# Two convolutional layers on one core: which bands of the last image have their third channel tile filtered on TensorE, and where the late taps stand

## The chip, the cores and the metric

The kernel runs on one core of one Trainium2 chip. The metric is the device time in microseconds of one execution; the figure given for a kernel is the median of its runs. The engines are called PE (TensorE's matrix multiply), PEld (its weight loads), DVE (VectorE), ACT (ScalarE), POOL (GpSimd) and SP (SyncE), as in the profile.

## The reference, cut to what matters

Eight images of 384 channels on a 64 x 64 grid pass through two layers, each added to its own input after a group normalisation:

```python
x = x + L0(gn(x), ...)   # linear attention with rotary positions
x = x + L1(gn(x), ...)
# L1:
t = einsum('bchw,oc->bohw', x, w_in)
t = irfft2(rfft2(8x8 blocks of t) * fft_filter)
t = conv 3x3, one filter for each channel (w_dw), zero padding
x1, x2 = t[:, :192], t[:, 192:]
out = einsum('bchw,oc->bohw', gelu(x1) * x2, w_out)
```

The edit concerns the 3 x 3 filter for each channel (the depthwise convolution) of the second layer in the last image.

## The kernel before, in words

All data are float32. The 384 channels lie in three tiles of 128 partitions. An image is cut into eight bands of eight rows (512 positions). For images 0 to 6 the second layer runs together with the keys of the next image; in the last image there is no next one, and a loop of its own (L1003 to L1023) runs over the eight bands. For each band j it calls, in this order:

- `expand_filter` (L618): the 1x1 convolution `w_in` on PE (`pi`, L624, 24 instructions in the profile), copies by ACT (`ht`, L631), the forward 8 x 8 transform on PE (`pd`, L638), and four multiplications by the filter on DVE (`tf`, L646).
- `normalised` for band j + 1 on ACT (`hf`, L332).
- `back_transform` (L649): the inverse transform on PE (`pb`, L659), copied by ACT into one of two ring buffers (L669). A ring buffer has ten rows, the band's eight and one on each side: row 0 is copied from the band before (L674), and row 9 of the band before is copied from this band's first row (L675). So a band's last row of filter taps can be made only when the next band has been transformed.
- `first_taps` (L702): tap k = 0 of each channel tile on ACT (L706).
- `contract` of band j - 2 (L779): the last 1x1 convolution `w_out` on PE (`pw`, L747 and L758), whose results ACT copies (`y`, L772) and POOL adds to the output by DMA (L777), or in the last band DVE adds (L774).
- `taps` of band j - 1 (L711): taps k = 1 to 8 on DVE (L720), one multiply-and-add of 128 x 512 for each tap and tile, 24 for a band. Taps 6 to 8 read row 9.
- `gate_taps` of band j - 1 (L722): GELU on ACT (L726, L730) and the product on DVE (L727, L731), into the single buffer `gated`, which must have been read by the `pw` of the band before.

For some bands (`on_array`, L681) the third channel tile is not filtered by ACT and DVE but by PE: nine matmuls with diagonal weights (`diagonals`, L685) add up in one PSUM bank (`ptap`, L694), and the gate reads that bank. In the kernel before these are bands 6 and 7 of the last image. Band 6's taps 0 to 5 stand in its `first_taps`, its taps 6 to 8 in `taps`, which is called after `first_taps` and `contract` of the next band; band 7 has all nine in `first_taps`. In the profile each of these matmuls is two instructions.

The calls above are not the order in which an engine works. A scheduler that runs when the program is built orders each engine's instructions by priority and by its own estimate of times, and so interleaves bands: each engine then runs its list in this fixed order, waiting where an operand isn't there. That list is part of the built program and can be read for both kernels without running them.

## Time and profile before

| | |
|---|---|
| runs | 3429.32, 3433.61, 3430.04 us |
| median | 3430.04 us |
| the profiled execution's own time | 3431.62 us |
| its span, first to last instruction | 3428.8 us |
| mean granted PE clock | 0.994 |
| last image's second layer (first `hf` to the last instruction of DVE) | 3248.8 to 3422.3 us |
| one DVE tap (L720), from one to the next when nothing is waited for | 0.667 us |
| taps on PE (L694), instructions | 36 |

The profile is of one execution, and its times are counted from the span's start. An engine's row gives how long it was busy; the arrow at a row's end names what ended the idle time before it. The granted clock is 1.00 when TensorE runs at full speed and 0.50 when it is held to half.

### The profile page before, as it was taken

Reading aid. Unit: us, or ns where it says so; the run is one execution under the profiler, and the core shown is the slowest. Engines: PE = TensorE matmul, PEld = TensorE weight load, DVE = VectorE, ACT = ScalarE, POOL = GpSimd, SP = SyncE. Lnnn points to the kernel's source line nnn. Section 1 sums busy time; section 2 is a strip of 40 time slices with the busy share of each in tenths; the row PEclk is TensorE's granted clock in tenths of the full one; section 3 lists DMA queues with packets and bytes.
Section 4 is the critical chain, followed back from the end, with each engine's and each line's share of the span. In section 5 each row is a group of like instructions: output and inputs, shape, how many; then the busy total and the mean of one; then the engine's idle time right before and its main releaser. Section 6 shows DMA issues by size and latency. Waiting matters only on the chain.

```text
span 3428.8 us, 50015 instructions
## 1 busy us (share of the span) xinstructions
PE 3337.2 (97%) x19760; PEld 1866.2 (54%) x19760; DVE 2801.2 (82%) x4396; ACT 1958.6 (57%) x3869; POOL 140.2 (4%) x247
## 2 busy tenths in 40 slices
PE   8999999999999999999999999999999999999988
PEld 5545555455654556545565455654556445564454
DVE  6586888869898698986989869897698967989598
ACT  4445666456655567545665557555576455554553
POOL 0000001000010000100001000010000000000000
PEclk9999999999999999999999999999999999999999
DMA  6323234333243333442343423334243331333113
GB/s 219 113 90 108 70 107 97 124 118 80 78 108 122 109 84 88 106 127 93 84 105 99 126 93 93 100 97 124 84 111 89 102 121 47 83 85 96 61 25 51
DMA packets 149328, 335.60 MB, mean 98 GB/s; under 512 B 27125, under 2 KB 38246, under 8 KB 140902
## 3 DMA queue, kind: packets, MB, share of 16 engines
q1 hardware_dynamic: 123702, 282.65, 24.8%
q0 software_dynamic: 25200, 49.55, 9.2%
q8 instruction: 155, 2.54, 0.3%
q14 instruction: 79, 0.65, 0.1%
q10 hardware_dynamic: 192, 0.21, 0.0%
HBM read 232.51 MB, written 99.88 MB: 97 GB/s over the span
## 4 chain that ended last, share of the span: by engine, by line
PE 64%; DVE 28%; ACT 5%; issue 2%; DMA 0%; SPq 0%; DVEq 0%; ACTq 0%
DVE dw L720 17%; PE pf L606 15%; PE pq L527 13%; PE acc L447 10%; PE pk L432 8%; PE pi L624 6%; PE pw L747 3%; PE pb L659 2%; DVE kc L439 2%; PE pd L638 2%; PE pw L758 1%; DVE kc L339 1%; DVE kc L435 1%; ACT ring L669 1%; PE pn L565 1%
## 5 line engine op out<-in xcount | busy, mean ns | idle before, releaser
L720 DVE SCALAR_TENSOR_TENSOR dw<-ring,w_dw,dw 128x512 f32<-128x512 f32 x1520 | 1061.4, 744 | 179.3 <-ACT ring L675 137.7
L432 PE MATMUL pk<-wk,x 128*128 128x384 f32 x1536 | 547.2, 495 | 8.7 <-DVE kc L435 8.7
L527 PE MATMUL pq<-x,wq 128*128 128x512 f32 x1152 | 520.8, 599 | 4.0 <-ACT qs L554 3.9
L606 PE MATMUL pf<-qc,mt 128*128 128x512 f32 x1152 | 513.6, 599 | 0.0
L624 PE MATMUL pi<-w_in,hf 128*128 128x384 f32 x1536 | 510.8, 489 | 2.1 <-ACT hf L332 1.3
L447 PE MATMUL acc<-xk,kc 128*128 128x385 f32 x1488 | 504.0, 492 | 0.0
L624 PEld LDWEIGHTS pi<-w_in,hf 128*128 128x128 f32 x1536 | 290.4, 191 | 204.9 <-issue 5.1
L447 PEld LDWEIGHTS acc<-xk,kc 128*128 128x128 f32 x1488 | 276.4, 190 | 204.5 <-issue 22.8
L432 PEld LDWEIGHTS pk<-wk,x 128*128 128x128 f32 x1536 | 278.1, 190 | 197.5 <-issue 22.8
L527 PEld LDWEIGHTS pq<-x,wq 128*128 128x128 f32 x1152 | 211.9, 190 | 255.1 <-issue 240.7
L606 PEld LDWEIGHTS pf<-qc,mt 128*128 128x128 f32 x1152 | 213.0, 190 | 250.0 <-issue 232.8
L399 ACT COPY xk<-px 128x384 f32<-128x384 f32 x248 | 118.1, 486 | 324.5 <-PE px L398 324.5
L631 ACT COPY ht<-pi 128x384 f32<-128x384 f32 x256 | 120.2, 479 | 235.7 <-PE pi L624 235.1
L610 DVE SCALAR_TENSOR_TENSOR x<-pf,bfc,x 128x512 f32<-128x512 f32 x192 | 140.9, 742 | 106.8 <-PE pf L606 106.2
L435 DVE TENSOR_TENSOR kc<-pk,kbias 128x384 f32<-128x384 f32 x256 | 141.2, 552 | 86.9 <-PE pk L432 85.6
L747 PE MATMUL pw<-gated,w_out 128*128 128x256 f32 x768 | 183.9, 386 | 5.7 <-DVE kc L435 5.6
L337 ACT ACTIVATE qs<-qc 128x1536 f32<-128x1536 f32 x64 | 95.0, 1484 | 158.0 <-DVE qc L556 148.0
L554 ACT ACTIVATE qs<-pq,qbias 64x512 f32<-64x512 f32 x128 | 87.3, 682 | 168.1 <-DVE qc L540 167.2
L179 ACT ACTIVATE differences<-x,shift 128x512 f32<-128x512 f32 x168 | 119.9, 714 | 77.1 <-DVE x L610 77.1
L777 POOL DMA_DIRECT2D out_dram<-y x63 | 80.7, 1281 | 2019.2 <-ACT y L772 1938.7
L669 ACT COPY ring<-pb 128x256 f32<-128x256 f32 x384 | 115.8, 406 | 81.3 <-PE pb L659 81.3
L747 PEld LDWEIGHTS pw<-gated,w_out 128*128 128x128 f32 x768 | 141.8, 192 | 33.6 <-DVE kc L435 11.3
(157 smaller groups left out, 4354.3 us busy)
## 6 DMA issues: line engine op xcount, KB each, us to landing
tq<-in_tq SPq DMA_DIRECT2D x64, 1024.0 KB, 4.8
x<-in_x SPq DMA_DIRECT2D x64, 768.0 KB, 6.3
tk<-in_tk SPq DMA_DIRECT2D x64, 768.0 KB, 4.5
out_dram<-x SPq DMA_DIRECT2D x63, 768.0 KB, 3.3
out_dram<-y POOLq DMA_DIRECT2D x63, 768.0 KB, 7.9
xs<-in_x SPq DMA_DIRECT2D x56, 768.0 KB, 5.8
wk<-in_wk SPq DMA_DIRECT2D x8, 576.0 KB, 3.9
wv<-in_wv SPq DMA_DIRECT2D x8, 576.0 KB, 3.7
```

Of the source, the lines that this page charges most:

```text
L179: nc.scalar.activation(out[:, m, :], x_[:, m, :], AF.Identity, bias=shift[:, m : m + 1], accum_out=of_m[0])
L432: nc.tensor.matmul(pk[:, :C], tokens(t), wks[:, t, :], start=(t == 0), stop=(t == CT - 1))
L435: nc.vector.tensor_add(kc[:, i, :], pk[:, :C], bias)
L447: nc.tensor.matmul(acc[m][:, : C + 1], kf[:, i, m * P : (m + 1) * P], xk[:, i, :], start=(j == 0 and i == 0), stop=(j == NBAND - 1 and i = ...
L527: nc.tensor.matmul(p_, wqs[:, t, m * P : (m + 1) * P], xt[b, j][:, t, :], start=(t == 0), stop=(t == CT - 1),)
L606: nc.tensor.matmul(p_, mt[:, t, m * P : (m + 1) * P], q[:, t, :], start=(t == 0), stop=(t == CT - 1))
L610: nc.vector.scalar_tensor_tensor(xm, p_, bfc[:, m : m + 1], xm, ALU.add, ALU.add)
L624: nc.tensor.matmul(p_[:, :C], h[:, t, i * P : (i + 1) * P], w_in[:, t, :], start=(t == 0), stop=(t == CT - 1),)
L631: nc.scalar.copy(ht[:, i, :], p_[:, :C])
L669: nc.scalar.copy(rows[:, u], ps[u][:, m - m0].rearrange("p s i (r c) -> p r s i c", r=8))
L720: nc.vector.scalar_tensor_tensor(acc[:, m], src, wd, acc[:, m], ALU.mult, ALU.add)
L747: nc.tensor.matmul(p_[h][:, m - m0, :], w_out[:, 0, m * P : (m + 1) * P], gated[:, h * HT : (h + 1) * HT], start=(m == m0), stop=False,)
```

## The change

Band 3 of the last image joins the bands whose third tile is filtered on PE. And the late taps (6 to 8) of such a band are called earlier: between `back_transform` and `first_taps` of the next band, so ahead of the next band's own taps, instead of in `taps`.

```diff
     def on_array(b, j):
 
-        return b == nb - 1 and j >= NBAND - 2
+        return b == nb - 1 and j in (3, NBAND - 2, NBAND - 1)
...
         t, acc = ring[j % 2], dw[b, j]
-        if on_array(b, j) and j < NBAND - 1:
-            array_taps(b, j, range(6, 9))
         for m in range(CT - on_array(b, j)):
...
         back_transform(b, j, tf[0])
+        if j and on_array(b, j - 1):
+
+            array_taps(b, j - 1, range(6, 9))
         first_taps(b, j)
         if j >= 2:
             contract(b, j - 2)
```

In the built order of the changed program, band 3's taps 0 to 5 stand on PE between its `pb` and `pw` of band 1; its taps 6 to 8 stand within `pw` of band 2. Band 6's taps 6 to 8 stand after the first of band 7's nine. On DVE, band 3 has 16 taps in place of 24; ten of them stand before `tf` of band 4 and six after it. Before `tf` of band 5 stand 15 taps of band 4, and before `tf` of band 6 stand nine of band 5's. The orders of POOL and SP are the same in both programs.

## The prediction

> **What bounds the kernel now.** I read the page first, then only the last image's second layer, since the edit acts from its band 3 on (after about 3310 us).

> ```profile
> PE 3337.2 (97%) x19760; PEld 1866.2 (54%) x19760; DVE 2801.2 (82%) x4396; ACT 1958.6 (57%) x3869; POOL 140.2 (4%) x247
> PE 64%; DVE 28%; ACT 5%; issue 2%; DMA 0%; SPq 0%; DVEq 0%; ACTq 0%
> ```

> PE bounds the whole, but the edited stretch may differ. Busy time by window (columns: PE, PEld, DVE, ACT, POOL, granted clock, DMA share, GB/s):

> ```profile
> 3268.00:3300.00 32.00, 28.31 (x299) 17.35 (x298) 30.82 (x50) 21.07 (x46) 1.28 (x1) 1.00 0.06 5
> 3300.00:3332.00 32.00, 26.00 (x284) 16.83 (x283) 31.82 (x53) 16.16 (x37) 1.28 (x1) 0.89 0.30 47
> 3332.00:3364.00 32.00, 29.62 (x211) 18.52 (x213) 31.78 (x51) 17.42 (x40) 2.55 (x2) 0.95 0.30 41
> 3396.00:3430.00 34.00, 23.24 (x96) 14.36 (x96) 19.69 (x32) 8.78 (x23) 2.83 (x3) 0.91 0.39 69
> ```

> Here DVE is full (31.8 of 32 us) until about 3367, then it is not. The DVE timeline tells what it waits for when it does wait:

> ```profile
> 3273.84 1.94 DVE L646 TENSOR_TENSOR tf<-pd,filt 128x384 f32<-128x384 f32 x4
> 3275.70 2.31 DVE L720 SCALAR_TENSOR_TENSOR dw<-ring,w_dw,dw 128x512 f32<-128x512 f32 x3
> 3279.00 6.05 DVE L720 SCALAR_TENSOR_TENSOR dw<-ring,w_dw,dw 128x512 f32<-128x512 f32 x9 [0.98 <-ACT ring L675]
> 3310.49 12.00 DVE L720 SCALAR_TENSOR_TENSOR dw<-ring,w_dw,dw 128x512 f32<-128x512 f32 x18
> ```

> Of a band's 24 taps (three tiles, k = 1 to 8), 15 need only the band itself; 9 (k = 6 to 8) need ring row 9, which L675 copies out of the next band. Here DVE had used up its 15 and waited. Row 9 is complete 5.13 us after the next band's tf started (3273.84 to 3278.97). A tap costs 12.00/18 = 0.667 us.

> The chain of waits after 3367 (us at, us long):

> ```profile
> 3366.99 0.57 DVE tf L646
> ...
> 3371.98 7.61 PE ptap L694 x12
> 3379.59 2.59 PE pw L747 x12
> 3382.18 1.50 PE pw L758 x12
> 3383.68 7.94 PE pi L624 x24
> 3391.61 0.89 PE pd L638 x8
> ...
> 3392.52 1.03 DVE tf L646 x2
> ...
> 3397.46 8.00 PE ptap L694 x18
> ```

> From the start of band 6's tf (3366.99) on, PE and its short hand-overs set the end. So the change is judged by one number: when does tf of band 6 start?

> [...]in the fence above nine taps stood still for row 9.[...] the granted clock was 0.50 in 3370 to 3374, and 12 tap matmuls took 7.61 us (634 ns each) against 18 in 8.00 us (444 ns) later.

> **Part 1: band 3's third tile to TensorE.** Removed: 8 DVE taps x 0.667 = 5.33 us and one ACT first tap (L706, 0.756; ACT has slack). Added: 9 taps = 18 matmul instructions x 0.444 = 8.0 us of PE, more when cold. Bank, ring and ptap gate reads (0.42 to 0.43 on DVE either way) cost nothing visible. POOL's and SP's orders are unchanged. Six of the taps stand between pb and pw of band 3; three stand among the pw of band 2, behind row 9. I walk the engine orders of the changed program with durations of the trace.

> Band 3. tf ends at 3310.57 as before. pb follows 0.94 later, ring copies (1.76), row 0 (0.24): ptap starts at 3313.55. PE has been idle some 2 us after small matmuls, as ahead of band 6's ptap[...]: 12 x 0.444 = 5.33 (low end), 7.61 (high end, as band 6's); taken 7.05, end 3320.6. Then the queue behind it: pw 2.59 + 1.50, pi 7.94, pd to tf 0.91: tf of band 4 can start at 3333.5. It started at 3327.34 in the trace.

> DVE meanwhile: 19 taps from 3310.49, the gate's multiply (held to 3323.9 by pw, then ACT's GELU), 4 taps, two half gates (0.9), then 7 taps of band 3: 3332.8. It waits 0.7 for tf, runs it (1.87), and has nothing left but band 3's six row-9 taps: 10 of 16 are done. Row 9 comes at 3333.5 + 5.13 = 3338.7. Stall: 3.3 us. This is the wait that takes the place of the removed taps; before, unfinished taps filled it.

> Band 4. 6 row-9 taps to 3342.7; a tap, the gate multiply (its GELU waits for pw of band 2, which PE ends at 3342.2 behind the three taps: just in time), 2 + 1 + 11 taps and two half gates: 3354.2. PE would have had tf of band 5 ready at 3343.7 + 7.94 + 0.91 = 3352.6, so DVE decides: tf at 3354.2 (before: 3347.04). All 15 own taps of band 4 are used up again. Row 9 at 3359.3; stall 3.3 us.

> Band 5. 7 row-9 taps, gate (0.6), 4 taps (2.67), half gates (0.9): 3368.1. Now the order puts **seven taps of band 5 ahead of tf of band 6** (in the kernel before there were only three of them before it). 7 x 0.667 = 4.67: tf starts at 3372.8, though PE is ready at 3370.1. Shift: 3372.8 - 3366.99 = 5.8. One tap stands amid the four tf: +0.67. Sum 6.5.

> Check by DVE's own account: -5.33 for 8 taps, +7.2 idle (0.7 at tf, twice 3.25 at row 9), six more taps of band 5 done before tf +4.0: +5.9.

> From here DVE's lead is worth nothing, because the PE chain follows tf at fixed distances: those six taps, done early, buy only idle time later (by this walk DVE is free at 3394.9 while tf of band 7 comes at 3399.0).

> **Part 2: the three taps of band 6 ahead of band 7's.** Before: ptap 8.00, pw 4.1, ptap 2.77, pw 4.1. After: 24 ptap instructions x 0.444 = 10.65, pw, pw: the same PE sum. What lay between pw of band 5 and of band 6 was cover for the gate of band 6 (GELU 0.63 after pw's L747 part, multiply 0.68). Without it these 1.35 us are covered by pw's L758 part (1.50) alone, and DVE has 6 + 15 taps from row 9 (14.0 us) in front of the multiply: pw of band 6 starts about 0.2 late. Between -0.1 and +1.0; taken +0.2.

> **Sum.** +6.5 + 0.2 = +6.7. Unknown: band 6's ptap warm (-2.3) or cold as before (0), taken -0.3; band 5's pb cold, row 9 late (0 to +0.5, band 4's was 5.67 in the trace), taken +0.3; hand-overs of about 0.04 on some eight steps that I left out, +0.3. Total +7.0. The profiled execution took 3431.62 (span 3428.8 and 2.8 around it), 1.6 over the median of 3430.04; its own sum would be 3438.6, and on the median the forecast is 3437.0.

> **Rivals.**
> 1. *The relief counts (faster).* DVE is full from 3268 to 3367 and 5.33 us leave it; if tf of band 6 comes earlier by that and PE then stays warm in its ptap (-2.3), the time is 3430.0 - 7.6 = 3422.4. It decides where tf of band 6 starts before 3366.99. Against it: row 9 can't come earlier than tf + 5.1, and PE has 8 us more to do between two tf with only 2 to 3.6 us of idle time in each band.
> 2. *PE becomes the bound, no more.* If DVE catches up and tf of band 6 starts when PE is ready (3370.1): +3.1 + 0.67 + 0.2 = +4.0, 3434.0. For it: ptap of band 3 warm pulls every later step 1.5 us forward. Against it: seven taps stand in front.
> 3. *All is hidden:* 3430. Speaks for it that the end is PE's chain; against it that this chain starts from the tf that moves.

> **Chances.** 0.2%, 6.9 us, is about what a measurement of this kernel can tell from no change; my forecast lies right at this line. Forecast mechanism 0.82 (+5 to +9: 0.52 over the line, 0.30 under it); rival 2 0.08 and rival 3 0.05, both within; rival 1 0.05, of which 0.04 by over 0.2% and 0.01 within. So faster 0.04, same 0.44, slower 0.52. The range takes both ptaps warm (+3) at its low end, and both fully cold with late rows and a spread of 1 to 2 us between runs at its high end (+10): 3433 to 3440.

> **What would show it.** Right: DVE idle for about 3 us ahead of six and of seven dw taps, released by ring L675; tf of bands 4, 5, 6 at about 3333.5, 3354, 3373; ptap of band 3 at about 3313.5 with a half clock in part; DVE busy falling well under 31.8 in 32 us between 3332 and 3364. Wrong: no such stalls, or tf of band 6 not later than 3369; then the walk missed slack on DVE. A ptap of band 6 at 5.3 us would alone take off 2.3.

## The result and the profile after

| | before | after |
|---|---|---|
| median of the compared runs (6 and 6) | 3431.28 us | 3443.74 us |
| lowest to highest | 3429.32 to 3433.61 us | 3442.71 to 3445.35 us |
| profiled execution's own time, span | 3431.62, 3428.8 us | 3443.7, 3441.9 us |

The changed kernel is slower by 12.5 us: ratio 1.0037, 95% interval 1.0025 to 1.0049. The forecast was +7.0, its range +3 to +10. The direction and the place were forecast, the size was not.

The two lines of the page that the prediction started from, for the changed kernel:

```profile
PE 3347.5 (97%) x19778; PEld 1869.5 (54%) x19778; DVE 2797.8 (81%) x4388; ACT 1962.8 (57%) x3868; POOL 140.3 (4%) x247
PE 64%; DVE 28%; ACT 5%; issue 2%; DMA 0%; SPq 0%; DVEq 0%; ACTq 0%
```

PE has 18 instructions more, as written, but 10.3 us more busy time (3347.5 against 3337.2). Eighteen at 0.444 us would be 8.0. DVE has eight instructions fewer. The shares of the chain are the same to the per cent: on the whole page the loss cannot be seen.

By stretch of time (columns as before: PE, PEld, DVE, ACT, POOL, granted clock, DMA share, GB/s):

```profile
3300.00:3332.00 32.00, 25.93 (x178) 15.34 (x177) 30.15 (x49) 11.86 (x27) 1.28 (x1) 0.84 0.22 28
3332.00:3364.00 32.00, 29.50 (x310) 18.07 (x308) 24.96 (x41) 18.68 (x42) 1.28 (x1) 1.00 0.29 47
3364.00:3396.00 32.00, 27.13 (x181) 15.69 (x180) 28.97 (x46) 13.23 (x31) 1.79 (x2) 0.84 0.17 25
3396.00:3430.00 34.00, 32.02 (x211) 18.73 (x210) 22.36 (x36) 11.32 (x28) 2.37 (x4) 0.95 0.25 32
```

DVE, full from 3332 to 3364 before (31.78), is now busy 24.96 us there: 6.8 us of new waiting. The clock is lower in the first row (0.84, it was 0.89). In the second it is full (0.95 before): the half clock has moved to other places.

The DVE timeline shows the waiting, row by row (start, length, what, how many, and in brackets the idle time before the row and what ended it):

```profile
3335.45 1.95 DVE L646 TENSOR_TENSOR tf<-pd,filt 128x384 f32<-128x384 f32 x4 [0.26 <-PE pd L638]
3340.62 4.72 DVE L718 SCALAR_TENSOR_TENSOR dw<-ring,w_dw,dw 128x512 f32<-128x512 f32 x7 [3.22 <-ACT ring L675]
3349.00 7.63 DVE L718 SCALAR_TENSOR_TENSOR dw<-ring,w_dw,dw 128x512 f32<-128x512 f32 x11
3356.66 1.95 DVE L646 TENSOR_TENSOR tf<-pd,filt 128x384 f32<-128x384 f32 x4
3361.84 4.72 DVE L718 SCALAR_TENSOR_TENSOR dw<-ring,w_dw,dw 128x512 f32<-128x512 f32 x7 [3.23 <-ACT ring L675]
3370.75 4.73 DVE L718 SCALAR_TENSOR_TENSOR dw<-ring,w_dw,dw 128x512 f32<-128x512 f32 x7
3375.39 1.02 DVE L646 TENSOR_TENSOR tf<-pd,filt 128x384 f32<-128x384 f32 x2
3402.80 1.95 DVE L646 TENSOR_TENSOR tf<-pd,filt 128x384 f32<-128x384 f32 x4 [3.58 <-PE pd L638]
```

The two stalls at row 9 are there, 3.22 and 3.23 us (forecast: 3.3 twice), and so are the seven taps ahead of tf of band 6, without a wait between them and it. The part that was wrong is found on PE. The chain of waits of the changed kernel:

```profile
3315.08 7.43 PE ptap L694 x12
3322.51 2.59 PE pw L745 x12
3325.11 1.50 PE pw L756 x12
3326.60 7.94 PE pi L624 x24
...
3381.53 8.34 PE ptap L694 x12
...
3407.74 12.27 PE ptap L694 x24
```

At full clock these three are 5.33, 5.33 and 10.65 us (0.444 us each). Together they are 6.7 us longer. The granted clock, cut into stretches of 3.4 us, shows why for the first of them:

```profile
3304.90:3308.30 3.40, 0.71 (x12) 0.04 (x4) 3.40 (x6) 0.49 (x1) 0.00 (x0) 1.00 0.01 1
3308.30:3311.70 3.40, 1.94 (x52) 1.75 (x56) 3.31 (x8) 2.25 (x4) 0.00 (x0) 0.59 0.00 0
3311.70:3315.10 3.40, 1.49 (x49) 1.30 (x49) 3.40 (x6) 2.09 (x8) 0.00 (x0) 0.50 0.02 5
3315.10:3318.50 3.40, 3.40 (x4) 1.48 (x5) 3.40 (x6) 1.41 (x3) 0.00 (x0) 0.50 0.00 0
```

PE is idle for most of the first stretch (busy for 0.71 of 3.40 us). The half clock begins 0.6 us into the second and lasts from 3308.94 to 3319.18, 10.24 us. The shortest spell of half clock in this trace (from 3407.92) lasts 3.41 us; counted in periods of that length it is three. PE is busy for 2.6, 1.5 and 3.4 us of these three: at first only with the 64 x 64 matmuls of `pb`, then with the end of `pb` and the start of `ptap`. Full clock comes back after the third, which is filled: three periods, not one. In the kernel before, the half clock begins behind the same wait (at 3308.16), but its first period is filled (3.36 of 3.41 us busy) and it lasts one, 3.41 us. PE timeline, before:

```profile
3308.21 1.85 PE L659 MATMUL pb<-idft,tf 64*64 64x64 f32 x48 [3.58 <-DVE tf L646]
3309.98 1.90 PE L747 MATMUL pw<-gated,w_out 128*128 128x256 f32 x4
3311.81 0.93 PE L659 MATMUL pb<-idft,tf 64*64 64x64 f32 x48
3312.67 2.00 PE L747 MATMUL pw<-gated,w_out 128*128 128x256 f32 x8
```

PE timeline, after:

```profile
3309.19 1.85 PE L659 MATMUL pb<-idft,tf 64*64 64x64 f32 x48 [3.58 <-DVE tf L646]
3311.61 1.56 PE L659 MATMUL pb<-idft,tf 64*64 64x64 f32 x48 [0.57 <-DVE tf L646]
3315.08 7.43 PE L694 MATMUL ptap<-ring,diagonals 128*128 128x512 f32 x12 [1.91 <-ACT ring L674]
```

The idle 3.58 us ahead of `pb` is the same in both. But before, `pw` of band 1 stood amid and behind `pb`. The second half of `pb` already ran at full rate (0.93), and nothing behind it was slow (24 `pi` in 8.01 us). In the changed order `ptap` stands between `pb` and that `pw`; the work that would have filled the wait now waits behind the slowed matmuls.

About one microsecond more is in the output. POOL's last two additions of `y` to the output, before:

```profile
3411.06 1.28 POOL L777 DMA_DIRECT2D out_dram<-y  x1 [13.57 <-ACT y L772]
3417.92 1.29 POOL L777 DMA_DIRECT2D out_dram<-y  x1 [5.58 <-ACT y L772]
```

and after:

```profile
3425.62 1.28 POOL L775 DMA_DIRECT2D out_dram<-y  x1 [17.84 <-ACT y L770]
3429.92 1.29 POOL L775 DMA_DIRECT2D out_dram<-y  x1 [3.03 <-ACT y L770]
```

They stand 6.86 us apart before and 4.30 after. The largest pieces of the last store of `x` (a row of the DMA issues: size of each, median us from issue to landing) take, before

```profile
out_dram<-x SPq DMA_DIRECT2D x2, 256.0 KB, 5.2
```

and after

```profile
out_dram<-x SPq DMA_DIRECT2D x2, 256.0 KB, 6.3
```

From the last band's first addition on DVE to the end of the span it is 8.5 us before and 9.6 after.

### The profile page after: what moved, and what is told of

It is laid out like the page before. It is cut to its first block, busy times and chain, and to the rows that moved or that the text cites. A ratio compares the mean times of both kernels' runs of the same rounds, so it can differ in the third digit from the quotient of the medians.

```text
span 3441.9 us, 50035 instructions
## 1 busy us (share of the span) xinstructions
PE 3347.5 (97%) x19778; PEld 1869.5 (54%) x19778; DVE 2797.8 (81%) x4388; ACT 1962.8 (57%) x3868; POOL 140.3 (4%) x247
## 4 chain that ended last, share of the span: by engine, by line
PE 64%; DVE 28%; ACT 5%; issue 2%; DMA 0%; SPq 0%; DVEq 0%; ACTq 0%
DVE dw L718 17%; PE pf L606 15%; PE pq L527 13%; PE acc L447 10%; PE pk L432 8%; PE pi L624 6%; PE pw L745 3%; DVE kc L439 2%; PE pd L638 2%; PE pb L659 2%; PE pw L756 1%; DVE kc L339 1%; ACT ring L669 1%; DVE kc L435 1%; PE pn L565 1%
## 5 line engine op out<-in xcount | busy, mean ns | idle before, releaser
L624 PE MATMUL pi<-w_in,hf 128*128 128x384 f32 x1536 | 510.6, 489 | 2.2 <-ACT hf L332 1.3
L624 PEld LDWEIGHTS pi<-w_in,hf 128*128 128x128 f32 x1536 | 290.3, 191 | 204.9 <-ACT hf L332 3.9
```

What stands on the lines that cost most here:

```text
L624: nc.tensor.matmul(p_[:, :C], h[:, t, i * P : (i + 1) * P], w_in[:, t, :], start=(t == 0), stop=(t == CT - 1),)
```

## The experiments

Each figure is the distance of a kernel's median from the median of the kernel before on the same chip (3430.5 to 3430.9 us in the four groups of runs). The changed kernel is at +12.5. In the traces I use one interval, from the start of tf of band 3 (just ahead of the first edited instruction) to the last band's first addition, since the runs differ by up to 2 us in when they reach it: 112.70 us before, 123.73 after. Where the interval of a ratio includes 1 (experiments 2, 3, 7, 8, 9 and 12), the runs alone do not tell the median from no change.

**1. Band 3 alone.** The late taps stay in `taps`.

```diff
-        return b == nb - 1 and j >= NBAND - 2
+        return b == nb - 1 and j in (3, NBAND - 2, NBAND - 1)
```

> Band 3's third tile is filtered on PE as in the change; the late taps stay where they stood before. My account (the change costs 12.5 us: 7.4 because tf of band 6 starts late, 3.6 in the PE chain behind it, 1.1 to 1.3 from the late taps' place, by way of the last two output DMAs): about 11 us slower than before. If the late taps' place carries most of the cost: at most 5 us slower.

Measured: 3442.29, +11.4; ratio 1.0032 (1.0020 to 1.0045). The interval is 123.77, as in the changed kernel. Nearly all of the cost is band 3.

**2. The late taps' place alone.**

```diff
     def taps(b, j):
-        if on_array(b, j) and j < NBAND - 1:
-            array_taps(b, j, range(6, 9))
...
         back_transform(b, j, tf[0])
+        if j and on_array(b, j - 1):
+            array_taps(b, j - 1, range(6, 9))
         first_taps(b, j)
```

> Bands 6 and 7 alone on PE as before; only band 6's late taps stand in front of band 7's. My account: 0 to 1.5 us slower than before, with the two last POOL DMAs issued some 4 us apart in place of 6.9. If the place carries most of the cost: 5 us or more slower.

Measured: 3432.28, +1.4; ratio 1.0004 (0.9995 to 1.0012): not told from nothing, though 11.4 and 1.4 add up nearly to what both parts cost. In the trace `pw` of band 6 starts late by just the sliver that was forecast, and waits for the gate:

```profile
3412.76 2.86 PE L745 MATMUL pw<-gated,w_out 128*128 128x256 f32 x12 [0.23 <-DVE gated L725]
```

POOL's last two additions are 4.59 us apart here, and the end comes 9.8 us after the first addition (before: 8.5).

**3. The relief without the load.** Band 3's third tile loses its eight taps on DVE and gets nothing on PE; that part of the filter is left out.

```diff
-        for m in range(CT - on_array(b, j)):
+        for m in range(CT - (on_array(b, j) or (b == nb - 1 and j == 3))):
             for k in range(1, 9):
```

> The kernel before, with the eight DVE taps of band 3's third tile left out and nothing added on PE (this part of the filter is missing). My account: the relief is worth little, since DVE's list then has seven taps of band 5 in front of tf of band 6 in place of three and idles for row 9: 1 to 3 us faster. If relief on DVE counts in full: 5.3 us faster. If PE alone sets the time: no change.

Measured: 3429.05, -1.8; ratio 0.9994 (0.9986 to 1.0002). Of 5.3 us taken off an engine that was busy 31.8 in 32 us, a third comes out at the end by the medians. The trace puts only 0.8 ahead of tf of band 6 (58.57 us from tf of band 3, 59.39 before). Its interval is 3.1 us shorter, but 2.2 of that is `ptap` of band 6, which runs at full clock in this trace (5.42 for 7.61) with nothing edited near it. The list of DVE is the scheduler's here too: from tf of band 3 to tf of band 6 it has 69 taps for 72 before, so that only three of the eight are gone ahead of tf of band 6. This is what the relief brings in that order, not in any order.

**4. The load without the relief.** In the changed kernel DVE and ACT still filter band 3's third tile; PE's 18 instructions run too, and no gate reads their bank.

```diff
-        for m in range(CT - on_array(b, j)):
+        for m in range(CT - (on_array(b, j) and j != 3)):
             for k in range(1, 9):
```

(and the same in `first_taps` and at the gate)

> The changed kernel, but DVE still does all 24 taps of band 3 and its gate uses these; the nine taps on PE are done for nothing. My account: DVE fills its waits for row 9 with the eight taps, so it is only about 2 us slower than the changed kernel (14 us slower than before). If relief counts in full: 5.3 us slower than the changed kernel (18 us slower than before).

Measured: 3444.01, +13.1; ratio 1.0037 (1.0024 to 1.0049). That is 0.6 over the changed kernel, and the runs of the two overlap. At the end the eight taps given up, 5.3 us of DVE, seem worth next to nothing. On the way they are worth more. The DVE timeline shows where they go:

```profile
3343.75 4.73 DVE L718 SCALAR_TENSOR_TENSOR dw<-ring,w_dw,dw 128x512 f32<-128x512 f32 x7 [3.75 <-ACT ring L675]
3365.11 4.73 DVE L718 SCALAR_TENSOR_TENSOR dw<-ring,w_dw,dw 128x512 f32<-128x512 f32 x7 [1.77 <-ACT ring L675]
```

DVE does more and waits less for row 9 of band 4 (1.77 for 3.23); it also uses 0.26 us of waiting at tf of band 4. But tf of band 6 comes 2.8 us later than in the changed kernel (69.64 us after tf of band 3 for 66.82). PE gives this back in this trace, because more of `ptap` of bands 6 and 7 is at full clock:

```profile
3384.01 7.22 PE L694 MATMUL ptap<-ring,diagonals 128*128 128x512 f32 x12 [1.67 <-ACT ring L674]
3409.11 10.57 PE L694 MATMUL ptap<-ring,diagonals 128*128 128x512 f32 x24 [1.77 <-ACT ring L674]
```

Against 8.34 and 12.27 in the changed kernel that is 2.8 us. So the relief is worth about half of its 5.3 us at tf of band 6 of the changed kernel, and the medians do not show it.

**5. tf of band 6 ahead of band 5's taps.** The scheduler is told to put those taps behind tf.

```diff
+            if j == NBAND - 2:
+                with tc.issue_after(last_tf[0]):
+                    taps(b, j - 1)
+            else:
+                taps(b, j - 1)
```

(`last_tf` is noted in `expand_filter`)

> The changed kernel, with band 5's taps issued on DVE behind tf of band 6. My account: tf of band 6 starts when PE's pd is ready, about 2.5 us earlier, and no tap stands amid its four: 3 us faster than the changed kernel (about 9.5 us slower than before). If PE's work alone sets the time, DVE's order is worth nothing: as the changed kernel.

Measured: 3440.57, +9.8; ratio 1.0029 (1.0018 to 1.0039). That is 2.7 us less than the changed kernel, and the runs of the two do not overlap. The order brings tf of band 6 forward by 2.2 us (64.57 us after tf of band 3 for 66.82). In this trace `ptap` of band 6 is at full clock as well (5.42 for 8.34), though nothing was added for it, so not all of the 2.7 need be the order. tf of band 6 now waits 2.98 us for PE:

```profile
3373.98 1.95 DVE L648 TENSOR_TENSOR tf<-pd,filt 128x384 f32<-128x384 f32 x4 [2.98 <-PE pd L640]
```

**6. The clock kept up.** To the changed kernel, matmuls whose result nobody reads are added in PE's waits: three behind `pd` of bands 3 and 6, two behind `pb` of bands 3, 6 and 7.

```diff
+    def warm(n):
+        ps = ps_tile("warm")
+        for _ in range(n):
+            ins = nc.tensor.matmul(ps[:, :C], w_in[:, 0, 0:P], w_in[:, 1, :], start=True, stop=True)
+            tc.keep_in_program_order(ins)
...
+        if j in (3, NBAND - 2):
+            warm(3)
...
+        if on_array(b, j):
+            warm(2)
```

> The changed kernel with idle matmuls (128x384, into a bank nobody reads) on PE: three behind pd of bands 3 and 6, two behind pb of bands 3, 6 and 7, where PE waits. If the half clock is what my sum missed, ptap takes 5.4 us in band 3 (7.4 in the changed kernel), 5.4 in band 6 (8.3) and 10.7 in band 7 (12.3): about 6 us faster than the changed kernel (6 us slower than before). If the cost is PE's work and the order alone: no faster than the changed kernel.

Measured: 3437.05, +6.3; ratio 1.0018 (1.0011 to 1.0025): half of the cost is gone with work added and none removed. Between the same points of the two traces it is 6.2 us (117.51 for 123.73), with the same number of DVE taps between each tf and the next. All three `ptap` run at full clock:

```profile
3314.33 5.42 PE L694 MATMUL ptap<-ring,diagonals 128*128 128x512 f32 x12 [0.17 <-ACT ring L674]
3379.42 5.42 PE L694 MATMUL ptap<-ring,diagonals 128*128 128x512 f32 x12 [0.17 <-ACT ring L674]
3402.71 10.57 PE L694 MATMUL ptap<-ring,diagonals 128*128 128x512 f32 x24 [0.28 <-ACT ring L674]
```

The same tap matmuls, slow for 2.0, 2.9 and 1.7 us in the changed kernel, make 6.6 us; the medians differ by 6.2 when each is taken from its own kernel before.

**7. The same cure in the kernel before.** Idle matmuls in bands 6 and 7 only, to tell whether they help where only band 6's `ptap` is slow (7.61 us; the diff is that of experiment 6, in bands 6 and 7).

> The kernel before with the same idle matmuls (bands 6 and 7). Its own half clock on the path is ptap of band 6, 7.6 us in place of 5.4: 2 us faster than before[...]. If the idle matmuls make a kernel faster by something else than the clock, they give as much here as in the changed kernel (6 us).

Measured: 3429.39, -1.2; ratio 0.9998 (0.9990 to 1.0006). `ptap` of band 6 falls from 7.61 to 5.42 and the interval by 1.7 (to 110.96). So here idle matmuls gain no more than they take off slowed tap matmuls; the 6.2 us of experiment 6 are not something that they bring to any kernel.

**8. Contract first.** In the kernel before, the tap matmuls of a band are issued behind `pw` of band j - 2.

```diff
             contract(b, j - 2)
+        if on_array(b, j):
+            array_taps(b, j, range(9 if j == NBAND - 1 else 6))
```

(taken out of `first_taps`)

> The kernel before, with the array taps of bands 6 and 7 behind pw of band j - 2, so that pw fills PE's wait for ring row 0. If PE's idle time and half clock in the tail count one for one: 1.67 + 1.77 + 2.28 = 5.7 us faster than before. By a walk of the lists DVE becomes late (its list ends only 0.1 us before tf of band 7 in the kernel before): about 2 us faster than before.

Measured: 3428.65, -2.1; ratio 0.9996 (0.9988 to 1.0004). `pw` fills the wait, `ptap` runs in 5.42 without an idle matmul, and the interval is 110.49.

**9. All nine taps of band 6 late.** In the kernel before they go behind `pb` of band 7.

```diff
         back_transform(b, j, tf[0])
+        if j and on_array(b, j - 1):
+            array_taps(b, j - 1, range(9))
```

(taken out of `first_taps` and `taps`; band 7's nine follow behind its `first_taps`)

> The kernel before, with all nine taps of band 6 behind pb of band 7. By a walk of the lists: tf of band 7 starts at about 3387 in place of 3392.5, and the PE chain behind it grows from 23.8 to some 27 us: 1 to 2 us faster than before, with ptap at full clock. If moving them buys nothing: as before.

Measured: 3430.48, -0.3; ratio 1.0000 (0.9992 to 1.0008). A miss: tf of band 7 is 5.3 us earlier (3387.23 for 3392.52), but 36 tap instructions then stand in one row of 15.7 us ahead of three `pw`, and the additions of `y` come 4.30 apart.

**10. All three cures in the changed kernel:** idle matmuls, tf of band 6 first, and band 6's late taps back in `taps` (the diffs of 5 and 6 together, and the late taps of band 6 alone moved back).

> The changed kernel with all three terms taken away at once: idle matmuls in PE's waits, band 5's taps behind tf of band 6 on DVE, band 6's late taps back in their old place. My account: the three add up nearly (6.7 measured for the idle matmuls, 2 to 3 for the order, 1.1 to 1.5 for the place), so about 1 to 3 us slower than before: band 3's taps on PE then cost what they relieve. If a further cost is hidden in band 3's filter on PE: 5 us slower or more. If the relief counts once the rest is gone: faster than before.

Measured: 3436.74, +6.2; ratio 1.0018 (1.0011 to 1.0026). A miss: no better than the idle matmuls alone. DVE's rows say why:

```profile
3371.68 1.95 DVE L648 TENSOR_TENSOR tf<-pd,filt 128x384 f32<-128x384 f32 x4 [3.00 <-PE pd L640]
...
3395.70 2.32 DVE L723 SCALAR_TENSOR_TENSOR dw<-ring,w_dw,dw 128x512 f32<-128x512 f32 x3
3397.94 1.94 DVE L648 TENSOR_TENSOR tf<-pd,filt 128x384 f32<-128x384 f32 x4
```

tf of band 6 comes 62.25 us after tf of band 3 (65.48 in experiment 6), so 3.2 were won. But tf of band 7 has no wait in front of it: DVE is the late one, because it now has the postponed taps to do between the two. In experiment 6 the same tf waited 3.10 us for PE. It comes at 88.51 and 89.42 us after tf of band 3: 0.9 of the 3.2 is left.

**11. Band 6's taps as filling.** In the kernel before, its nine taps are issued where PE waits: three behind `pd` of band 7, six behind `pw` of band 5.

```diff
         run(layer1)
+        if j == NBAND - 1:
+            array_taps(b, j - 1, range(3), True)
...
             contract(b, j - 2)
+        if j == NBAND - 1:
+            array_taps(b, j - 1, range(3, 9))
+            array_taps(b, j, range(9))
```

(taken out of `first_taps` and `taps`)

> The kernel before, with band 6's nine taps used to fill PE's waits: three behind pd of band 7, six behind pw of band 5 and in front of band 7's nine. From the run with all nine late (tf of band 7 at 3387.2, then 2.35 us of PE idle and two output DMAs 4.3 us apart): 2 us less for the filled wait and 1 us less for the DMAs, about 3 us faster than before.

Measured: 3426.43, -4.1; ratio 0.9989 (0.9982 to 0.9995): faster than both kernels, with the same instructions as before. PE timeline:

```profile
3383.99 2.84 PE L694 MATMUL ptap<-ring,diagonals 128*128 128x512 f32 x6
...
3394.88 13.14 PE L694 MATMUL ptap<-ring,diagonals 128*128 128x512 f32 x30
```

No `ptap` waits, and none is slow (13.14/30 = 0.438).

**12. Band 3 as filling too:** experiment 11 and band 3's nine taps in the same way.

```diff
-        return b == nb - 1 and j >= NBAND - 2
+        return b == nb - 1 and j in (3, NBAND - 2, NBAND - 1)
...
-        if j == NBAND - 1:
+        if j in (4, NBAND - 1):
             array_taps(b, j - 1, range(3), True)
```

(and in the same way behind `contract`)

> The kernel with band 6's taps as filling (3426.4 us), and band 3's third tile on PE as well, its nine taps as filling too: three behind pd of band 4, where PE waits for DVE, six behind pw of band 2. The work on each engine is that of the changed kernel. My account: it is the place of the taps ahead of pi of band 4 that made the change dear; here tf of band 4 starts on time, one wait for row 9 (3.2 us) is left, tf of band 6 is 1 to 2 us late and DVE is six taps further by then: within 1 us of 3426.4. If eight microseconds more of PE work cost as such: 8 us slower than 3426.4. If the relief counts: 5 us faster.

Measured: 3428.86, -2.0; ratio 0.9994 (0.9986 to 1.0003). 2.4 over the median of experiment 11 (2.1 when each is taken from its own kernel before), where I expected at most 1. Of the two new stalls at row 9 one is left on DVE, that of band 4:

```profile
3355.88 4.73 DVE L719 SCALAR_TENSOR_TENSOR dw<-ring,w_dw,dw 128x512 f32<-128x512 f32 x7 [3.39 <-ACT ring L675]
```

and tf of band 6 comes 2.7 us later, counted from tf of band 3, than before (62.13 for 59.39). But the work is that of the changed kernel, tap for tap, and it is 14.5 us faster (+12.5 against -2.0). The cost lay in where the tap matmuls stood, with what followed from it in the scheduler's list for DVE: 23 taps stand there between tf of bands 3 and 4, as before, and 30 in the changed kernel. The 8.0 us of PE work as such, put into its waits, cost about 2 us over experiment 11, with the relief of DVE counted in.

## Why the prediction was right in kind and wrong in size

Its own milestones, each as a shift against the trace of before. The changed kernel's trace is late by 0.97 us already at tf of band 3; that is taken off.

| start of | forecast | measured | miss that arises here |
|---|---|---|---|
| tf of band 4 | +6.2 | +7.1 | 0.9, clock |
| tf of band 5 | +7.2 | +8.7 | 0.6, DVE's hand-overs |
| tf of band 6 | +5.8 | +7.4 | 0.1 |
| tf of band 7 | +6.5 | +9.3 | 1.2, clock |
| last band's addition | +6.7 | +11.0 | 1.5, clock |
| end of the span | +6.7 | +12.1 | 1.1, output |

The misses sum to 5.4. The forecast had another net 0.3 for unknowns, which leaves 5.1 between its +7.0 and the 12.1 of this pair of traces.

**What held.** The walk of DVE: the stalls at row 9 (3.3 twice; measured 3.22, 3.23), the seven taps ahead of tf of band 6 (experiment 5: moving them back brings it forward by 2.2 us), a relief that does not pay for the load (experiments 3 and 4: 0.8 us at tf of band 6 without the load, 2.8 with it, of 5.3), the second part's +0.2 on PE (experiment 2: 0.23). These are right in mechanism and nearly in size.

**The step that failed is the clock.** "PE has been idle some 2 us after small matmuls, as ahead of band 6's ptap ... taken 7.05". The 7.05 us are 1.72 over the 5.33 at full clock: half clock for 3.4 us, one period, which was my estimate. I took over that count from another place in another order, and misread it there: in the kernel before, the half clock at band 6 lasts from 3369.60 to 3376.43, 6.83 us, which is two periods. In band 3 the idle time ahead of `pb` was already there in the kernel before, 3.58 us, and the half clock behind it lasted one period only, with `pw` of band 1 right behind the first half of `pb`. The change puts `ptap` ahead of that `pw` (the prediction's "between pb and pw of band 3" names the wrong band) and so removes the filling. What that can cost stood in the trace of before: the period at band 6 with 1.74 us of PE was followed by another of half clock, the one at band 3 with 3.36 us was not. In experiment 12 `pw` stands there again, and the second half of `pb` takes 0.93 us as before. In the changed kernel `ptap`, its start and `pb` are slow: 0.9 us more than taken.

"Band 6's ptap warm (-2.3) or cold as before (0), taken -0.3" had the wrong sign. It became 8.34 (before 7.61), and `pb` in front of it lost 0.5. And "24 ptap instructions x 0.444 = 10.65" has no clock term at all: 12.27 was measured. These terms are the 3.6 of the table. In these two bands no filling was taken away: the wait ahead of `ptap` of band 7 is 1.77 us in both kernels. What differs in the traces is how the work falls on the periods of 3.41 us, counted from the edges of the half clock: the one ahead of that `ptap` has 1.64 us of PE in the changed kernel and 2.07 in the kernel before, and only the first was followed by half clock. The forecast could not know which it would be; it went wrong in taking both terms as nothing or less.

Experiment 6 shows that the clock is the cause, and not only beside it: at full clock, with everything else in place, 6.2 of the 12.5 us go. It is more than 3.6 because the forecast had counted 1.7 for band 3 already, and 2.2 in band 6 were in the kernel before too. These make 7.5; other waits take some of it back (2.1 us gained at tf of band 5 are 1.3 at tf of band 6).

The traces of before and after show more of the half clock than my sum used. From 3260 to 3420 us its spells last 3.41, 6.83 or 10.24 us and start whole multiples of 3.41 us apart: in the changed kernel they last 10.24, 10.24 and 3.41 us (from 3308.94, 3377.20 and 3407.92) and start 20 and 9 times 3.41 us apart. Some work in the period ahead did not keep it away: PE was busy for 1.64 us of the one ahead of the last of these spells. And the same matmuls were slowed in one trace and not in another: `ptap` of band 6 took 7.61 us in the kernel before and 5.42 in experiment 2, where nothing ahead of it is edited. By this difference (2.2 us), a sum with such a term needs a range of some 2 us for each `ptap` that stands behind a wait of PE. There were three such places in the changed kernel, and my high end of +10 had room for two.

**The term that was missing is the output.** "After: ... the same PE sum" is true, but PE's sum is not the end: the additions of `y` move together. That they are the cause rests on a comparison only. In the six traces in which POOL's last two additions are 4.3 to 4.6 us apart (after, and experiments 2, 4, 5, 6, 9), the end comes 9.35 to 10.05 us after the last band's first addition; where they are some 6.9 or more apart (before, 1, 3, 7, 8, 10, 11, 12) it is 8.15 to 9.0. No run changed this spacing alone.

**One statement held only where it was made.** "From here DVE's lead is worth nothing, because the PE chain follows tf at fixed distances". In the changed kernel that is so (tf of band 7 waits 3.58 us for PE). Experiment 10 shortens PE's chain by the clock and takes DVE's lead away, and there DVE ends last. The three savings, 6.2, 2.7 and 1.1, don't add.

**The rivals.** The first (faster) falls with the result, in which tf of band 6 is late, and with experiments 3 and 4: the relief brings tf of band 6 forward by 0.8 us alone and by 2.8 in the changed kernel, too little for the load either way. The second (PE's readiness sets tf of band 6) is what experiment 5 makes, and it costs +9.8, not +4.0: PE is itself late by then (tf of band 6 is at +5.2, not +3.1). The third falls with the result.

What stays open: in experiment 10 about 6 us of cost remain. The trace shows tf of band 6 2.9 us late (62.25 for 59.39) with two stalls of 3.21 us at row 9 ahead of it. From there to the last addition it is another 1.4 (54.75 for 53.31), with DVE late at tf of band 7. That is 4.3; the other 2 us lie ahead of tf of band 3, which this trace reaches 1.8 us later than before, and which no edit touches. I can't assign these 2 us: the traces of experiments 2 and 8 also reach that point 2.2 and 2.1 us later than before, with medians of +1.4 and -2.1.

The half-clock spells themselves are seen only in the profiled executions, but the mean granted clock of each run is on record. It was 0.992 or 0.993 in all six runs of the changed kernel, 0.994 or 0.995 in all 128 runs of the kernel before that the experiments are measured against, and 0.995 or 0.996 in all 20 of experiment 6, so the longer half clock of the changed kernel is no accident of one trace. And in the kernel before, in each of the four groups, the runs at 0.994 take 1.0 to 1.6 us longer by their median than those at 0.995: a part of the spread of one kernel's runs goes with the clock.

## What to carry to other kernels

When work is moved onto the array, look at what stands behind it in PE's list: if it is put between a wait and the matmuls that used to follow that wait, it can run at half clock, as `ptap` of band 3 did for a part (7.43 us for 5.33), and it delays those matmuls as well. Put such work into the waits themselves, which here was worth 14.5 us with the same work. Full busy rows of the engine that is relieved say little; ask which of its waits the removed work was hiding.
